# A graph layer and an LSTM on one core: one square root changes places with one copy in ScalarE's queue

## The chip, the cores and the metric

The kernel runs on one core of a Trainium2 chip. The core has five engines that each work through a queue of their own in order: TensorE (PE in the profile, its weight loads PEld), VectorE (DVE), ScalarE (ACT), GpSimd (POOL) and SyncE (SP). They wait for each other by semaphores. Transfers (DMA) are issued from the queues and run beside them. TensorE writes its results to PSUM, from where VectorE and ScalarE read them; all other tiles lie in SBUF.

The metric is the device time of one execution in microseconds (us), the median over the runs shown; less is better.

## The reference

`x` holds 1250 nodes with 512 features, `src` and `dst` 20000 edges, sorted by `dst`. A two-layer graph network on the normalised rows is added to `x`, then an LSTM that walks over the nodes in order:

```python
def _gcn2_layer(h, h0, src, dst, norm, w1, w2, b, layer):
    beta = float(np.log(LAMBDA / layer + 1.0))
    x = h * norm
    agg = jax.ops.segment_sum(x[src], dst, num_segments=h.shape[0])
    agg = agg * norm
    f = agg * (1.0 - ALPHA)
    f0 = h0 * ALPHA
    rst = (1.0 - beta) * f + beta * (f @ w1) + (1.0 - beta) * f0 + beta * (f0 @ w2) + b
    return jax.nn.relu(rst)
...
    h = feat @ fc_w.T + fc_b
    deg = jax.ops.segment_sum(jnp.ones_like(dst, dtype=h.dtype), dst, num_segments=n)
    norm = jnp.clip(deg, 1.0, None) ** (-0.5)
...
    x = x + _L0_gnn_ref(_layernorm(x, axis=-1), src, dst, ...)
    x = x + _L0_ffn_ref(_layernorm(x, axis=-1)[None], ...)[0]
```

`_layernorm` takes the mean off each row and divides by sqrt(var + 1e-5). What matters here is the beginning: the layer norm of `x`, the product `h` with `fc_w`, and the products of `h` with `w2` of both layers, which are the parts `f0 @ w2` and `(1 - beta) * f0 + b`.

## The kernel before

The 1250 rows are laid out as 10 tiles of 128 rows (T = 10, R = 128), each of 512 features.

The work has three stages. The *first stage* (L294 to L560, up to about 183 us in the profile) does two things side by side: it makes layer norm, `h` and the products with `w2` for each tile, and it counts the edges into an adjacency matrix. The *second stage* (`layers`, L797) is the aggregation with that matrix, twice. The *third* (`lstm`, L925) is the recurrence. The change touches the first stage alone.

In the first stage TensorE, VectorE and ScalarE carry out exactly the order in which the code is written (`tc.manual_schedule` at L341): on each engine an instruction starts only when all that were written before it for that engine have started, and when what it needs is there. The loop `for s in range(T + 3)` at L500 writes the stage in portions. One portion works on several tiles at different steps. Portion s = 4, the fifth, writes in this order (before the change):

- `transposed(...)` (L507): TensorE turns the normalised rows of tile 4 by four transposes into a PSUM tile (L169, `psT`), and ScalarE copies it to SBUF as `xT` (L174).
- `stats(5, 7)` and `scales(5, 7)` (L510, L511): VectorE takes mean and variance of tiles 5 and 6 (L157, L158) and adds eps (L162, `ln_v`); ScalarE takes the square root (L88, `ln_s`); VectorE refines its inverse in five small operations (L90 to L95) and makes `nmr`, minus the mean over the deviation (L354). `rsqrt` is at L84, its tiles are of their own for each call.
- `normed(5)` (L513): ScalarE writes the normalised rows of tile 5 (L362).
- `add_base(0)` (L517, L498): VectorE adds the biases to the two products of tile 0 with `w2`, from PSUM into `base1` and `x2`. The pool `psM` has two buffers, and both hold these products until then.
- `count(c0)` (L519): a batch of edges. For each group of 125 edges VectorE has made two one-hot tiles (L434, L436, eight buffers of each); TensorE multiplies them into a PSUM block (L450, with a first zero product L447 for a new block). VectorE makes the one-hots of a batch two batches on. A finished block is cast by ScalarE (L289).
- `product(..., fcT)` (L521, L180): TensorE multiplies `xT` of tile 3 with `fc_w` into the next buffer of `psM`, the one that held the first product of tile 0.
- further batches, the transposes and the copy of `h` of tile 2 (`hT`, L524), the bias of `h` (L526), and the two products of tile 1 with `w2` (L548, L554).

In portion s = 1 the same two calls stand at the same place for tiles 2 and 3. Portions 1 and 5 have further statistics behind their counts (L528). The sizes of the batches per portion are in `per_slot` (L486).

Of the kernel before, what the change touches and what calls it, by code (L numbers as in the profile page):

```python
# [38 lines left out]
def gnn_lstm_kernel(  # L39
# [115 lines left out]
    def layernorm_stats(pool, mv, t, rows):  # L155
        st = pool.tile([R, 6], F32, name="bnst")
        nc.vector.bn_stats(st, rows)  # L157
        nc.vector.bn_aggr(mv[:, t, :], st)  # L158

    def layernorm_scale(pool, mv, out, name, times=1.0):  # L160
        ve = pool.tile([R, mv.shape[1]], F32, name=name + "_v")
        nc.vector.tensor_scalar(ve, mv[:, :, 1], EPS, None, OP.add)  # L162
        rsqrt(pool, ve, out, name, times)
# [8 lines left out]
    def transposed(pool, ps, rows, name):  # L172
        o = pool.tile([128, KD, R], F32, name=name)
        nc.scalar.copy(o, transpose_in(ps, rows))  # L174
        return o

    def product(ps, lT, rhs, name="psM"):
        p = ps.tile([R, D], F32, name=name)
        for k in range(KD):
            nc.tensor.matmul(p, lT[:, k, :], rhs[:, k, :], start=(k == 0), stop=(k == KD - 1))  # L180
        return p
# [32 lines left out]
    with ExitStack() as gnn_stack:  # L214
# [20 lines left out]
        def most_edges():  # L235
            nc.vector.tensor_reduce(most, S.rearrange("b i r -> b (i r)"),
                                    mybir.AxisListType.X, OP.max)
            nc.vector.tensor_scalar(most, most, 256.0, None, OP.is_gt)

        def row_totals():  # L240
            nc.vector.tensor_reduce(row, deg, mybir.AxisListType.X, OP.add)
            nc.vector.tensor_sub(row, row, most)

        def total(pn):
            nc.tensor.matmul(pn, row, ones, start=True, stop=True)
            nc.vector.tensor_scalar(missing, pn, -1.0, float(E), OP.mult, OP.add)
# [38 lines left out]
        def close_block(p, i, dst):  # L285

            nc.scalar.copy(dst, p.rearrange("b (i q a) -> b a i q", i=T, a=T))  # L289
            nc.vector.tensor_reduce(S[:, :, 4 * i:4 * i + 4],  # L290
                                    dst.rearrange("b a i q -> b i q a"),
                                    mybir.AxisListType.X, OP.add)

        with tc.tile_pool(name="prep", bufs=1) as prep, \  # L294
# [46 lines left out]
            with tc.manual_schedule(engines={mybir.EngineType.PE, mybir.EngineType.DVE,  # L341
# [6 lines left out]
                def stats(t0, t1):  # L348
                    for t in range(t0, t1):
                        layernorm_stats(work, mv, t, xt[:, t, :])  # L350

                def scales(t0, t1):
                    layernorm_scale(prep, mv[:, t0:t1, :], rstd[:, t0:t1], f"ln{t0}")
                    nc.vector.scalar_tensor_tensor(nmr[:, t0:t1], mv[:, t0:t1, 0], -1.0,  # L354
                                                   rstd[:, t0:t1], op0=OP.mult, op1=OP.mult)
# [3 lines left out]
                def normed(t):  # L359
                    if t < T:  # L360
                        xns[t] = work.tile([R, D], F32, name="xn")
                        nc.scalar.activation(xns[t], xt[:, t, :], AF.Identity,  # L362
                                             bias=nmr[:, t:t + 1], scale=rstd[:, t:t + 1])
# [76 lines left out]
                def count_group(c):  # L440
                    lo, hi = spans[c]
                    ob, od = hot.pop(c)
                    done = []
                    for i in range(lo // BW, (hi - 1) // BW + 1):
                        if i not in blocks:
                            blocks[i] = acc.tile([R, D], F32, name="acc")[:, :BW * T]
                            nc.tensor.matmul(blocks[i], none[:, :R], none, start=True, stop=False)  # L447
                        d0, d1 = max(lo, i * BW), min(hi, (i + 1) * BW)
                        last = all((i + 1) * BW <= a for a, b in spans[c + 1:])
                        nc.tensor.matmul(blocks[i][:, (d0 - i * BW) * T:(d1 - i * BW) * T], ob,  # L450
                                         od[:, (d0 - lo) * T:(d1 - lo) * T],
                                         start=False, stop=last)
                        if last:
                            done.append((blocks.pop(i), i))
                    return done
# [5 lines left out]
                def onehots(n):  # L461
                    for c in range(n * BATCH, min((n + 1) * BATCH, EC)):
                        make_onehot(c)

                def count(batches):
                    nonlocal counted
                    for n in range(counted, counted + batches):
                        closed = []
                        for c in range(n * BATCH, (n + 1) * BATCH):
                            closed += count_group(c)  # L470
                        onehots(n + 2)
                        for p, i in closed:
                            close_block(p, i, adj[:, :, :, 4 * i:4 * i + 4])
                    counted += batches
# [15 lines left out]
                def scale_w2(l):  # L490
                    nc.scalar.activation(w2[l], w2[l], AF.Copy, scale=ALPHA * betas[l])

                def add_w2(l):
                    add_identity(w2[l], ALPHA * (1.0 - betas[l]))

                def add_base(t):
                    for l, p in enumerate(ps_b.pop(t)):
                        nc.vector.tensor_add(base[l][:, t, :], p, bl[l])  # L498

                for s in range(T + 3):  # L500
                    c0, c1, c2 = per_slot[s] if s < len(per_slot) else (0, 0, 0)
                    if 0 < s < 3:

                        ps_h[s - 1] = product(psM, xTs.pop(s - 1), fcT)
                        count(c0)
                    if 0 < s < T:
                        xTs[s] = transposed(work, psT, xns.pop(s), "xT")  # L507
                    if s in (1, 4):
                        t0 = 2 if s == 1 else 5
                        stats(t0, t0 + 2)  # L510
                        scales(t0, t0 + 2)  # L511
                    if s:
                        normed(s + 1)  # L513
                    if s == 2:
                        scale_w2(0)
                    if 0 <= s - 4 < T - 3:
                        add_base(s - 4)  # L517
                    if s >= 3:
                        count(c0)  # L519
                        if s - 1 < T:  # L520
                            ps_h[s - 1] = product(psM, xTs.pop(s - 1), fcT)  # L521
                    count(c1)
                    if 0 <= s - 2 < T:
                        hTs[s - 2] = transposed(prep2, psT, h[:, s - 2, :], "hT")  # L524
                    if 0 <= s - 1 < T:
                        nc.vector.tensor_add(h[:, s - 1, :], ps_h.pop(s - 1), fcb)  # L526
                    count(c2)
                    if s in (1, 5):  # L528

                        t0, t1 = (4, 5) if s == 1 else (7, T)  # L530
                        stats(t0, t1)
                        scales(t0, t1)
                    if s == 2:
                        scale_w2(1)
                        add_w2(0)
                        add_w2(1)
                    if 0 <= s - 3 < T:


                        hT = hTs.pop(s - 3)  # L540
                        ps, name = (psM, "psM") if s < T + 1 else (acc, "acc")
                        if s == T + 1:
                            total(psT.tile([128, KD, R], F32, name="psT")[:1, 0, :1])
                            split_first(prep2, order[3:7])
                        if s == T + 2:
                            add_base(T - 2)
                            split_first(prep2, order[7:9])
                        ps_b[s - 3] = [product(ps, hT, w2[0], name)]  # L548
                        if s == T:
                            most_edges()  # L550
                            count_edges(psT.tile([128, KD, R], F32, name="psT")[:, 0, :])
                            row_totals()
                            degree_norm(prep)
                        ps_b[s - 3].append(product(ps, hT, w2[1], name))  # L554
                        if s == T:
                            add_base(T - 3)
                            split_first(prep2, order[:3])
# [643 lines left out]
```

## Time and profile before

| | us |
|---|---|
| runs | 1070.84, 1070.83, 1069.89; median 1070.83 |
| profiled execution: its own time | 1068.22 |
| profiled execution: span from first to last instruction | 1066.3 |
| TensorE busy | 1002.9 |
| VectorE busy | 533.3 |
| ScalarE busy | 327.9 |
| mean granted TensorE clock | 0.992 |

A row of the timeline reads: start in us, duration in us, engine, line, operation, tile written <- tiles read, shape, number of instructions merged, and in brackets the idle time of the engine just before with the instruction that ended it. "The chain that ended last" is followed back from the end of the execution: at each step to what released an instruction, or to the instruction before it on its engine. Busy times of merged TensorE rows overlap by some tenths of a us with the next row, since matmuls are pipelined.

### The profile page before, as it was taken

The page shows a single profiled execution, that of the slowest core. Times are in us where ns is not written, and L with a number is a line of the kernel's source. Part 1 is how long each engine was busy: PE and PEld are TensorE (multiplying, and loading weights), DVE is VectorE, ACT ScalarE, POOL GpSimd, SP SyncE. Part 2 cuts the span into 40 slices and gives each one's busy share as a digit, 9 for nine tenths or more (in the row PEclk, how much of TensorE's full clock was granted, in tenths as well). Part 3 has the DMA queues.
Part 4 walks back from the last instruction along what each step waited for, and adds up shares of the span by engine and source line. Part 5 has one row for each costly group of instructions (what it writes and reads, how often), then busy time and mean ns, then how long its engine had stood idle before and what let it go on. Part 6 is the DMA issues. An engine that isn't in the chain of part 4 may idle for free.

```text
span 1066.3 us, 26042 instructions
## 1 busy us (share of the span) xinstructions
PE 1002.9 (94%) x10988; PEld 519.0 (49%) x10988; DVE 533.3 (50%) x1915; ACT 327.9 (31%) x1012; POOL 79.5 (7%) x119
## 2 busy tenths in 40 slices
PE   6899999999999999999999989999999999999996
PEld 4455554554455443344444444544544544454453
DVE  7888877003400665665555444444444444445444
ACT  3312224213410124443333333333333333333332
POOL 1100000520000001111010144000000000000000
PEclk9899999999999999999999999999999999999999
DMA  8200001600200045853333356333333333434441
GB/s 220 89 1 1 1 1 50 231 1 20 77 1 1 0 109 175 247 163 116 106 120 105 120 147 175 93 91 97 100 90 94 102 92 91 122 84 121 113 107 22
DMA packets 38223, 98.48 MB, mean 92 GB/s; under 512 B 5796, under 2 KB 11756, under 8 KB 38094
## 3 DMA queue, kind: packets, MB, share of 16 engines
q1 hardware_dynamic: 28208, 68.67, 23.9%
q0 software_dynamic: 7168, 23.60, 6.6%
q10 hardware_dynamic: 2718, 4.42, 1.6%
q8 instruction: 89, 1.46, 0.6%
q14 instruction: 40, 0.33, 0.1%
HBM read 74.29 MB, written 19.76 MB: 88 GB/s over the span
## 4 chain that ended last, share of the span: by engine, by line
PE 70%; DVE 14%; ACT 8%; issue 3%; DMA 3%; SPq 1%; POOL 0%; ACTq 0%; DVEq 0%; POOLq 0%
PE gates L654 30%; PE psM L180 15%; PE agg L816 12%; PE psM L1008 8%; ACT adj L661 3%; PE acc L450 3%; DVE adj L664 3%; ACT adj L672 3%; DVE hT L688 3%; DVE adj L667 2%; DVE adj L673 2%; DMA h<-xp_d 1%; PE gates L646 1%; DMA xp_d<-planes 1%; PE psT L169 1%
## 5 line engine op out<-in xcount | busy, mean ns | idle before, releaser
L654 PE MATMUL gates<-Wh,hT 128*32 128x256 f32 x7936 | 453.6, 380 | 38.4 <-DVE hT L688 38.4
L654 PEld LDWEIGHTS gates<-Wh,hT 128*32 128x32 f32 x7936 | 232.9, 109 | 230.8 <-DVE hT L688 78.6
L664 DVE SCALAR_TENSOR_TENSOR adj<-adj 128x128 f32<-128x128 f32 (+1 forms) x260 | 76.6, 295 | 215.0 <-ACT adj L661 215.0
L1008 PE MATMUL psM<-Wx,xT 128*128 128x512 f32 x320 | 147.7, 607 | 0.0
L661 ACT ACTIVATE adj<-gates 128x192 f32<-128x192 f32 x248 | 81.7, 329 | 207.6 <-PE gates L654 198.5
L816 PE MATMUL agg<-adj,planes 128*128 128x512 bf16 x720 | 130.1, 344 | 1.9 <-DVE x L498 1.9
L672 ACT ACTIVATE adj<-adj 128x64 f32<-128x64 f32 (+1 forms) x249 | 63.9, 257 | 126.0 <-DVE adj L667 126.0
L816 PEld LDWEIGHTS <-planes 128*128 128x128 bf16 x720 | 70.4, 98 | 62.4 <-DVE x L498 2.7
L673 DVE SCALAR_TENSOR_TENSOR adj<-adj 128x64 f32<-128x64 f32 (+1 forms) x249 | 56.3, 226 | 80.5 <-ACT adj L672 80.5
L1008 PEld LDWEIGHTS psM<-Wx,xT 128*128 128x128 f32 x320 | 58.6, 191 | 70.7 <-issue 70.0
L688 DVE STREAM_TRANSPOSE hT<-adj 128x64 f32<-128x64 f32 x248 | 60.9, 246 | 8.5
L667 DVE SCALAR_TENSOR_TENSOR adj<-adj 128x64 f32<-128x64 f32 (+1 forms) x260 | 59.4, 228 | 8.9
L180 PE MATMUL psM<-w,hT 128*128 128x512 f32 x128 | 58.6, 610 | 0.0
L1028 POOL DMA_DIRECT2D xp_d<-planes x40 | 29.2, 731 | 375.8 <-DVE planes L1027 232.8
L436 DVE TENSOR_SCALAR od<-ids,key 125x820 f16<-125x820 f16 (+42 forms) x160 | 56.9, 356 | 0.0
L663 ACT ACTIVATE adj<-gates 128x64 f32<-128x64 f32 x248 | 54.0, 218 | 0.0
L646 PE MATMUL gates<-h,sel 96*32 96x256 bf16 x992 | 49.9, 273 | 0.0
L450 PE MATMUL acc<-od,ob 125*128 125x400 f16 (+22 forms) x360 | 46.4, 260 | 3.0 <-DVE od L436 2.7
L434 DVE TENSOR_SCALAR ob<-ids,low 125x128 f16<-125x128 f16 x160 | 40.6, 254 | 10.3 <-PE acc L450 10.1
L646 PEld LDWEIGHTS <-sel 96*32 96x32 bf16 x992 | 26.5, 97 | 34.9 <-issue 15.9
L1020 ACT CAST planes<-adj 128x512 bf16<-128x512 f32 x40 | 24.7, 618 | 60.4 <-DVE adj L1018 60.4
L598 DVE SCALAR_TENSOR_TENSOR r<-psM,norm,base 128x512 f32<-128x512 f32 x10 | 7.5, 751 | 71.4 <-PE psM L180 71.4
(163 smaller groups left out, 720.4 us busy)
## 6 DMA issues: line engine op xcount, KB each, us to landing
h<-xp_d SPq DMA_DIRECT2D x136, 384.0 KB, 4.1
xp_d<-planes POOLq DMA_DIRECT2D x40, 384.0 KB, 3.5
base<-x POOLq DMA_DIRECT2D x40, 64.0 KB, 4.9
w<-in_L_gnn_w_dram SPq DMA_DIRECT2D x2, 1024.0 KB
w<-in_L_gnn_w_dram POOLq DMA_DIRECT2D x2, 1024.0 KB, 6.4
xp_d<-planes SPq DMA_DIRECT2D x10, 144.0 KB, 3.5
h<-in_x_dram SPq DMA_DIRECT2D x10, 128.0 KB, 2.7
h<-in_x_dram SPq DMA_DIRECT2D x10, 120.0 KB, 4.1
```

Of the source, the lines that this page charges most:

```text
L180: nc.tensor.matmul(p, lT[:, k, :], rhs[:, k, :], start=(k == 0), stop=(k == KD - 1))
L450: nc.tensor.matmul(blocks[i][:, (d0 - i * BW) * T:(d1 - i * BW) * T], ob, od[:, (d0 - lo) * T:(d1 - lo) * T], start=False, stop=last)
L646: nc.tensor.matmul(ps[s][32 * j:32 * (j + 1), :, :], lhs(j), rhs(j, s), start=True, stop=False)
L654: nc.tensor.matmul(ps[s][32 * j:32 * (j + 1), :, :], hT[b // 2][:, b % 2, :], Wh[:, b, :, 128 * j + 64 * s:128 * j + 64 * (s + 1)], start= ...
L661: nc.scalar.activation(cg[:, 1:4, :], p[:, 0:3, :], AF.Tanh, scale=0.25)
L664: nc.vector.scalar_tensor_tensor(pr, cg[:, 1:3, :], 1.0, cg[:, 0:4:3, :], op0=OP.add, op1=OP.mult)
L667: nc.vector.scalar_tensor_tensor(then[:, 0, :], pr[:, 0, :], 0.5, pr[:, 1, :], op0=OP.mult, op1=OP.add)
L672: nc.scalar.activation(th, cg[:, 0, :], AF.Tanh, scale=0.5)
L673: nc.vector.scalar_tensor_tensor(hh, so, 1.0, th, op0=OP.add, op1=OP.mult)
L688: nc.vector.transpose(hT.rearrange("p b c -> p (b c)"), hh[:, m])
L816: nc.tensor.matmul(p[:, :n * R], planes[:, k, pl, f * 128:(f + 1) * 128], adj[:, k, t0:t0 + n, :].rearrange("b i r -> b (i r)"), start=(k ...
L1008: nc.tensor.matmul(p, yT[n][:, k, :], quarter(Wx[:, k, :, :], j), start=(k == 0), stop=(k == KD - 1))
```

## The change

In portion s = 4 the calls `stats(5, 7)` and `scales(5, 7)` are written ahead of `transposed(...)` instead of behind it. In portion s = 1 nothing changes.

```diff
@@ -503,12 +503,15 @@
 
                         ps_h[s - 1] = product(psM, xTs.pop(s - 1), fcT)
                         count(c0)
+                    if s == 4:
+
+                        stats(5, 7)
+                        scales(5, 7)
                     if 0 < s < T:
                         xTs[s] = transposed(work, psT, xns.pop(s), "xT")
-                    if s in (1, 4):
-                        t0 = 2 if s == 1 else 5
-                        stats(t0, t0 + 2)
-                        scales(t0, t0 + 2)
+                    if s == 1:
+                        stats(2, 4)
+                        scales(2, 4)
                     if s:
                         normed(s + 1)
                     if s == 2:
```

The transposes are TensorE's, and the statistics VectorE's; ScalarE is the only engine that has work in both parts. So the two programs differ in one place of one queue, ScalarE's (besides line numbers):

```diff
 L174 TensorCopy hT<-psT 128x512
-L174 TensorCopy xT<-psT 128x512
 L88 Activation ln_s<-ln_v 128x2
+L174 TensorCopy xT<-psT 128x512
 L362 Activation xn<-base,nmr,rstd 128x512
```

Lines behind L516 have a number higher by 3 in the changed kernel.

## The prediction

> **What bounds the kernel now.** I read the page's busy times and slices first, then the shares of the chain that ended last.
>
> ```profile
> PE 1002.9 (94%) x10988; PEld 519.0 (49%) x10988; DVE 533.3 (50%) x1915; ACT 327.9 (31%) x1012; POOL 79.5 (7%) x119
> ...
> PE   6899999999999999999999989999999999999996
> ...
> PE 70%; DVE 14%; ACT 8%; issue 3%; DMA 3%; SPq 1%; POOL 0%; ACTq 0%; DVEq 0%; POOLq 0%
> ```
>
> TensorE is busy 94% of the span, so a step elsewhere counts only where TensorE stands still for it. The edit lies in the first stage, in the portion s = 4 of the loop at L500. Its place in time is where the fifth copy to xT (tile 4) and the square root of tiles 5 and 6 run, near 44 us. So the next view is the chain in order of time there (start, duration, what):
>
> ```profile
> 43.48 0.45 PE psT L169 x4
> ...
> 44.01 0.58 ACT xT L174
> 44.59 0.11 ACT ln_s L88
> ...
> 44.73 0.18 DVE ln_r L90
> ...
> 45.80 0.70 DVE base L498
> ...
> 46.54 3.70 PE psM L180 x8
> ```
>
> This is the whole case: for 2.6 us the chain leaves TensorE. It goes from the transposes through ScalarE's copy and the square root, through VectorE's six small operations (L90 to L354), then the sum of `base`, and only then back to a product. The timeline of all engines shows who stood idle, in brackets:
>
> ```profile
> 42.19 0.17 DVE L162 TENSOR_SCALAR ln_v<-mv 128x2 f32<-128x2 f32 x1
> ...
> 44.01 0.58 ACT L174 COPY xT<-psT 128x512 f32<-128x512 f32 x1 [7.42 <-PE psT L169]
> 44.13 0.42 PE L450 MATMUL acc<-od,ob 125*128 125x20 f16 x5
> 44.49 0.21 ACT L88 ACTIVATE ln_s<-ln_v 128x2 f32<-128x2 f32 x1
> 44.73 0.17 DVE L90 RECIPROCAL ln_r<-ln_s 128x2 f32<-128x2 f32 x1 [2.37 <-ACT ln_s L88]
> ...
> 46.54 3.70 PE L180 MATMUL psM<-fcT,xT 128*128 128x512 f32 x8 [1.99 <-DVE base L498]
> ```
>
> The input of the square root (ln_v, L162) is ready at 42.36. ScalarE is idle then, but the head of its queue is the copy, which waits for transposes that TensorE begins only at 43.31. VectorE waits 2.37 us for a square root that could have run, and TensorE 1.99 us for VectorE: the product of tile 3 writes the PSUM buffer that the sum into `base` (add_base(0), L498) still has to read, since psM has two.
>
> **The change part by part.** Nothing is added or removed. On TensorE, VectorE, GpSimd and SyncE every instruction keeps its place. On ScalarE alone the square root of tiles 5 and 6 (L88) goes from behind the copy to xT to in front of it. The moved lines issue no DMA and pass no queue but ScalarE's.
>
> *The square root earlier.* Where nothing stands before it, it follows ln_v at once, as tiles 7 to 9 show:
>
> ```profile
> 74.34 0.17 DVE L162 TENSOR_SCALAR ln_v<-mv 128x3 f32<-128x3 f32 x1
> ...
> 74.78 0.17 DVE L90 RECIPROCAL ln_r<-ln_s 128x3 f32<-128x3 f32 x1 [0.27 <-ACT ln_s L88]
> ```
>
> From the start of ln_v to the reciprocal that is 0.44 us. So the reciprocal moves from 44.73 to 42.19 + 0.44 = 42.63, by 2.10 us. From there to the product VectorE's work is unchanged (44.73 to 46.54, 1.81 us), so the buffer is free at 44.44 instead of 46.54. The sum into `base` would start at 43.70; the matmuls it reads are the first half of the sixteen that ran from 36.60 to 43.48, done near 40.0. The second sum, into x2, would start at 44.31, after 43.48 as it must.
>
> *TensorE.* It has work of its own (the counts of L450) to 44.13 + 0.42 = 44.55. So the product starts when both are done. By the gate alone the gain is 2.10. By the recorded idle time it is 1.99. By the chain without a stop (the next tile's product, 60.81 to 64.30, takes 3.49 from the end of the counts) the product would end at 48.04 instead of 50.25 (46.54 + 3.70 in the chain): 2.21. Ends 1.99 and 2.21; I take 2.10, which lies between and is set by the gate.
>
> *The copy behind the square root.* This is the added wait: queued behind the square root on ScalarE are the copy to xT, the scaled rows of tile 5 (L362), the cast at 50.70 and the copy to hT at 52.08. The square root would run from 42.40 to 42.61, in idle time of ScalarE, 1.3 us before the transposes are done, so the copy still starts at 44.01 and the price is nothing. If that cover went (statistics late by more than 1.4 us), the copy's reader is the product at 60.64, sixteen us later, so it would still cost nothing. The rows of tile 5 move from 45.98 to about 44.5; they are transposed at 59.3.
>
> *New neighbours.* The sum into `base` now runs beside the copy to xT, both reading PSUM. No row has just this pair. The sum took 0.69 beside the scaled rows at 45.80 and 0.68 alone at 56.54. I bound it at -0.01 and +0.1 us (a hundredth between those rows, times ten for the untried pair) and take 0.
>
> *What is late next.* From 46.54 to 167 TensorE has no wait worth a line; VectorE waits for it instead (1.81 us at 50.41, 2.32 at 59.54, 1.88 at 64.53), so it can follow 2.10 us earlier. DMA share is 0.00 to 0.01 between 36 and 160 us, so no transfer with a time of its own can hold the shift. The weights of later stages are requested when the last planes are written (GpSimd waited 145.8 us for those), so they shift too.
>
> *The clock.* TensorE's granted clock in stretches (columns: stretch, its length, busy times by engine, clock, DMA share, GB/s):
>
> ```profile
> 25.00:30.00 5.00, 2.41 (x13) 1.81 (x14) 4.56 (x24) 4.71 (x6) 1.59 (x4) 0.54 1.05 390
> 30.00:32.00 2.00, 2.00 (x4) 0.97 (x4) 2.00 (x9) 2.00 (x3) 1.63 (x5) 0.50 1.03 370
> ...
> 44.00:48.00 4.00, 2.01 (x12) 1.03 (x10) 3.10 (x14) 1.50 (x3) 0.00 (x0) 1.00 0.00 2
> 48.00:52.00 4.00, 4.00 (x28) 2.46 (x27) 2.19 (x13) 0.49 (x1) 0.00 (x0) 1.00 0.00 0
> ```
>
> A stop of 2.18 us before 26.82 was followed by half clock to 32; the stop of 1.99 us in our portion was not followed by any. At half clock a product of eight takes 5.25 (at 161.77) instead of 3.49: 1.76 more. So in this execution the clock adds 0 to the gain. The Trainium skill, "TensorE: Matmul & The Clock Gate" (What's actually happening), states that the clock is halved after an idle window of about 3.4 us, that the window runs freely, and that where the work falls in it varies from run to run. The trace agrees in that half clock and full clock both follow stops of about 2 us; by that rule the stop would cost the clock in some executions and not in others.
>
> *Sum.* 2.10 + 0 + 0 + 0 = 2.10 us. The profiled execution took 1068.22 us (span 1066.3 and 1.92 around it) and would take 1066.1, its span 1064.2. The median of the runs, 1070.83, is 2.61 above it; I take the same difference off the median: 1070.83 - 2.10 = 1068.7.
>
> **The rivals.**
>
> 1. *The stop costs the clock too.* If in the usual execution half clock follows the stop at 44.55, it goes with the stop: 1070.83 - 2.10 - 1.76 = 1067.0. For: the same length of stop did it at 26.8, and the runs are 2.6 us above the execution whose clock held. Against: the clock row at 44 to 52 is 1.00.
> 2. *Given back later, or never had.* One more half-clock product behind the change (there is one at 161.77, where 20 matmuls of one column ran before it) costs 1.76 of the 2.10: 1070.5. Or the square root does not start earlier: 1070.8. Against the latter: it writes a tile of its own and reads only ln_v.
> 3. *Slower: the aggregation stage entered cold.* TensorE stops 1.90 us before 183.40, and the change shifts this stop by 2.1 us against whatever sets the clock. Half clock there costs half its length. A stretch as long as that from 25.7 to 32.1 costs 3.2, time 1071.9; it decides from 4.2 us on (slower than before), and slower by 0.2% needs 8.5 us. For: stops of this length have been followed by half clock. Against: the longest stretch in the trace is 6.4 us, and full clock holds from 183 to 376.
> 4. *Slower by ScalarE's queue*: the square root holds the copy to xT. It starts to cost when the statistics end later than about 58 us (the product at 60.64, less 2.1 and the copy's 0.58). Every us behind that costs one, and 1073.0 would need them near 62, twenty us late, while VectorE works without a break from 34.79 to 42.36. Hardly possible.
>
> **How the numbers follow.** What a measurement of this kernel tells from no change is about 0.2%, 2.14 us: just what I forecast, so the first two classes split the main case. Main case (gap closes, 1068.7, own range 1068.0 to 1069.4 from the ends 1.99 and 2.21 and half a us of scatter between runs, which lie 0.9 apart): 0.70. Rival 1: 0.14; 2: 0.11; 3: 0.04; 4: 0.01. Faster by over 0.2%: 0.40 of the main case, as its bound of 2.21 lies beyond the line, and rival 1, together 0.54. Within 0.2%: the other 0.30 and rival 2, 0.41. Slower: 0.05. The range takes in rival 1 and the weaker part of rival 2, 1066.8 to 1070.2, and leaves out the full giving back, the slower cases and the tails.
>
> **What would show it.** Right: the square root of tiles 5 and 6 starts 0.2 us after ln_v and 1.3 us before the copy; the reciprocal's wait of 2.37 falls to about 0.3; TensorE's wait of 1.99 for `base` falls under 0.15; the product ends 2.1 us earlier relative to the transposes of tile 4; and the aggregation's first matmul comes as much earlier. Wrong: the wait for `base` stays, or a new one of about 2 us appears between 46 and 183 us, or the aggregation starts earlier and the end does not.

## The result, and the profile after

The changed kernel took 1066.96 us (median of 20 runs, 1063.32 to 1070.56), the kernel before 1070.03 us (20 runs, 1067.34 to 1074.06). The ratio is 0.9976 with a 95% interval of 0.9965 to 0.9987, so 2.6 us faster, between 1.4 and 3.7. The prediction was 1068.7 within 1066.8 to 1070.2, faster by 2.10 us.

The profiled execution of the changed kernel took 1065.37 us, its span is 1063.3 us. Busy times, slices and chain shares of its page:

```profile
PE 1001.9 (94%) x10988; PEld 519.2 (49%) x10988; DVE 532.9 (50%) x1915; ACT 327.6 (31%) x1012; POOL 79.5 (7%) x119
...
PE   7999999999999998999999989999999999999996
...
PE 71%; DVE 14%; ACT 7%; DMA 3%; issue 3%; SPq 1%; POOL 0%; ACTq 0%; DVEq 0%; POOLq 0%
```

No engine has less work; one wait is gone. The chain in order of time at the place of the change (start, duration, what) no longer leaves TensorE:

```profile
43.50 0.44 PE psT L169 x4
43.94 0.21 PE acc L450 x2
44.15 0.17 PE acc L447
44.32 0.26 PE acc L450 x5
44.58 3.59 PE psM L180 x8
48.16 0.94 PE acc L450 x11
```

The timeline of the changed kernel shows why:

```profile
42.21 0.17 DVE L162 TENSOR_SCALAR ln_v<-mv 128x2 f32<-128x2 f32 x1
42.41 0.20 ACT L88 ACTIVATE ln_s<-ln_v 128x2 f32<-128x2 f32 x1 [5.80 <-DVE ln_v L162]
...
42.65 0.17 DVE L90 RECIPROCAL ln_r<-ln_s 128x2 f32<-128x2 f32 x1 [0.27 <-ACT ln_s L88]
...
43.72 0.69 DVE L498 TENSOR_TENSOR base<-psM,b 128x512 f32<-128x512 f32 x1
...
44.03 0.58 ACT L174 COPY xT<-psT 128x512 f32<-128x512 f32 x1 [1.41 <-PE psT L169]
44.15 0.42 PE L450 MATMUL acc<-od,ob 125*128 125x20 f16 x5
44.33 0.68 DVE L498 TENSOR_TENSOR x<-psM,b 128x512 f32<-128x512 f32 x1
...
44.46 3.70 PE L180 MATMUL psM<-fcT,xT 128*128 128x512 f32 x8
```

The square root starts 0.20 us after ln_v and 1.6 us before the copy, VectorE's wait for it falls from 2.37 to 0.27 us, and the product of tile 3 has no wait in brackets at all. From the first transpose of tile 4 to the end of the product of tile 3 it is 4.66 us (43.50 to 48.16); before it was 6.77 (43.48 to 50.25). That is 2.11 us.

The aggregation starts at 179.60 us instead of 183.40, by 3.80 us. 2.09 of these are the change; most of the rest is a product behind it: the eight passes that took 5.25 us at 161.77 before take 3.56 at 159.69. The clock in stretches tells (columns: stretch, its length, busy times by engine, granted clock, DMA share, GB/s). Before:

```profile
156.00:160.00 4.00, 4.00 (x15) 1.89 (x14) 3.97 (x6) 1.07 (x3) 0.00 (x0) 1.00 0.00 0
160.00:164.00 4.00, 4.00 (x19) 2.58 (x20) 2.67 (x13) 0.41 (x2) 0.00 (x0) 0.74 0.02 4
164.00:168.00 4.00, 4.00 (x13) 1.93 (x12) 1.52 (x3) 1.14 (x2) 0.00 (x0) 0.84 0.00 0
```

After:

```profile
156.00:160.00 4.00, 4.00 (x25) 2.91 (x24) 3.12 (x6) 0.00 (x0) 0.00 (x0) 1.00 0.01 4
160.00:164.00 4.00, 4.00 (x15) 2.01 (x14) 2.73 (x12) 1.55 (x3) 0.00 (x0) 1.00 0.00 0
```

So one pair of executions mixes the change with the clock. From the aggregation to the end the two are alike: 882.9 us before, 883.7 after. Two questions are left for the experiments: is it really the held PSUM buffer, and does the stop cost the clock as well (the first rival)?

### The profile page after: what moved, and what is told of

Its sections match the earlier page's. It is cut to its first block, busy times and chain, and to the rows that moved or that the text cites. A ratio compares the mean times of both kernels' runs of the same rounds, so it can differ in the third digit from the quotient of the medians.

```text
span 1063.3 us, 26042 instructions
## 1 busy us (share of the span) xinstructions
PE 1001.9 (94%) x10988; PEld 519.2 (49%) x10988; DVE 532.9 (50%) x1915; ACT 327.6 (31%) x1012; POOL 79.5 (7%) x119
## 4 chain that ended last, share of the span: by engine, by line
PE 71%; DVE 14%; ACT 7%; DMA 3%; issue 3%; SPq 1%; POOL 0%; ACTq 0%; DVEq 0%; POOLq 0%
PE gates L657 30%; PE psM L180 14%; PE agg L819 12%; PE psM L1011 8%; ACT adj L664 3%; PE acc L450 3%; DVE adj L667 3%; ACT adj L675 3%; DVE hT L691 3%; DVE adj L670 2%; DVE adj L676 2%; DMA h<-xp_d 1%; DMA xp_d<-planes 1%; PE gates L649 1%; DMA base<-in_x_dram 1%
```

## The experiments

The runs used several chips, so each ratio is against runs of the kernel before on the same chip. Four experiments (sums first, square root held back, stop filled, portion 1 too) share one chip and its runs of the kernel before; the changed kernel itself was not run on that chip, so a comparison with it is one of ratios from two chips. "Section" is the time from the first transpose of tile 4 to the end of the product of tile 3, by the chain or the timeline of the run's profile.

**The sums first, the square root left where it was.**

```diff
                         stats(t0, t0 + 2)
+                        if s == 4:
+                            add_base(0)
                         scales(t0, t0 + 2)
...
-                    if 0 <= s - 4 < T - 3:
+                    if 0 < s - 4 < T - 3:
                         add_base(s - 4)
```

> The kernel before, with the square root left behind the copy to xT; instead the two sums of tile 0 (add_base(0)) are written between the statistics and the scales of portion 4, so VectorE does them before it waits for the square root. Theory (the price of the old order is the PSUM buffer that the sum into base holds): the sum runs near 42.2 us, the product of tile 3 follows the counts without a stop, TensorE's idle 1.99 us goes, the product ends 2.1 us earlier against the transposes of tile 4, and the time falls as with the change, by 2.1 us (0.2%). The square root still starts about 44.5 and the rows of tile 5 about 46. Rival (the gain came from the rows of tile 5 or from ScalarE's order): no gain, 1070.

Measured: ratio 0.9959 (0.9941 to 0.9977), 4.4 us faster (2.5 to 6.3), so more than the 2.1 us expected. Its timeline:

```profile
42.51 0.67 DVE L498 TENSOR_TENSOR base<-psM,b 128x512 f32<-128x512 f32 x1
...
44.44 0.59 ACT L174 COPY xT<-psT 128x512 f32<-128x512 f32 x1 [7.42 <-PE psT L169]
...
44.57 0.43 PE L450 MATMUL acc<-od,ob 125*128 125x20 f16 x5
...
44.83 3.66 PE L180 MATMUL psM<-fcT,xT 128*128 128x512 f32 x8
44.92 0.21 ACT L88 ACTIVATE ln_s<-ln_v 128x2 f32<-128x2 f32 x1
```

The square root still runs behind the copy, the rows of tile 5 start at 46.41 as late as ever, and yet TensorE's stop is gone; the section is 4.58 us. So TensorE's stop in the old order came from the buffer that the sum into `base` holds, and from nothing else that hangs on the square root. Why the whole time fell by more than the stop is not shown by this run.

**The square root held back in the new order.** Three passes of ScalarE stand between ln_v and the square root.

```diff
-                        scales(5, 7)
+                        scales(5, 7, [xt[:, 5, :]] * 3)
...
+        for n, r in enumerate(rows):
+            nc.scalar.activation(h[:, 7 + n, :], r, AF.Identity, bias=v[:, 0:1])
         nc.scalar.activation(s, v, AF.Sqrt)
```

> The changed kernel with three extra passes of ScalarE over a tile between ln_v and the square root (each 0.8 us, 0.71 from start to start; they write rows of h that are overwritten later). Theory (each us of the square root is a us of TensorE): the square root starts 2.13 us later, near 44.55, the product of tile 3 starts near 46.6, TensorE's stop is back at 2.0 us, and the time is that of the kernel before (within 0.2%), although the order is that of the changed kernel. Rival (the order matters by itself, or the gain was luck of the clock): the time stays that of the changed kernel, 2 to 2.6 us under before.

```profile
43.18 0.17 DVE L164 TENSOR_SCALAR ln_v<-mv 128x2 f32<-128x2 f32 x1
43.39 1.95 ACT L88 ACTIVATE h<-base,ln_v 128x512 f32<-128x512 f32 x3 [5.80 <-DVE ln_v L164]
...
45.24 0.19 ACT L90 ACTIVATE ln_s<-ln_v 128x2 f32<-128x2 f32 x1
...
47.27 1.98 PE L182 MATMUL psM<-fcT,xT 128*128 128x512 f32 x4 [1.72 <-DVE base L500]
```

The three passes took 1.85 us instead of 2.13, and the product starts 4.09 us after ln_v instead of 2.25 in the changed kernel: 1.84 later. So at this place each us of the square root is a us of TensorE, and the order by itself does not close the stop. The whole time was a miss: expected like before, measured 0.9973 (0.9957 to 0.9989), 2.9 us faster (1.2 to 4.6), with a stop of 1.72 us where before has 1.99. That is the time that the rival named. The profile speaks against the order as its cause, since the stop is back; a stop that is 0.27 us shorter and that no half clock follows would give about 1 us by the estimate below, near the lower end of the interval. The rest stays open.

**The stop filled in the old order.** TensorE multiplies the identity while it waits.

```diff
                         count(c0)
+                        if s == 4:
+                            p = psT.tile([128, KD, R], F32, name="psT")
+                            for n in range(8):
+                                nc.tensor.matmul(p[:, 0, :], ident, ident, start=True, stop=True)
```

> The kernel before, with eight products of the identity with itself written behind the counts of portion 4, into a free PSUM buffer: TensorE works through its stop of 1.99 us, and nothing else moves. Theory (the wait itself is the price): the product of tile 3 still starts near 46.5, the time is that of before within 0.1%. Rival (the stop costs the clock): the mean granted clock rises and the time falls by up to 1.8 us, without the product of tile 3 starting earlier.

Measured, by the chain (first and third row) and the timeline:

```profile
44.62 0.45 PE psT L169 x4
45.53 2.01 PE L523 MATMUL psT<-ident 128*128 128x128 f32 x16
47.68 3.70 PE psM L180 x8
```

The product starts no earlier (section 6.76 us, as before; a product of the identity is two rows of the profile, so eight are x16), but the ratio is 0.9974 (0.9959 to 0.999), 2.8 us faster (1.1 to 4.4), and the mean granted clock of the runs is 0.9925 against 0.9906 of before on that chip. This is the rival's sign, though more than its 1.8 us, which the interval holds. The theory that the time stays within 0.1% falls.

**The kernel before, profiled three more times.**

> The kernel before once more, for its profile: does half clock follow the stop of portion 4 in some executions? So far filling the stop raised the mean granted clock from 0.9906 to 0.9925, about 4 us less at half clock, although the product of tile 3 started no earlier. The clock record shows stretches of 3.41 us on a grid that lies anew in each execution. Theory A (the stop costs the clock where one stretch of the grid holds most of it): in about half of the executions a stretch at half clock begins between 46.5 and 50 us and costs up to 1.7 us. Theory B (the stop never costs the clock, the means differ by scatter): full clock from 36 to 60 in all.

> As for the run ahead of it: theory A expects a stretch at half clock between 46.5 and 53 us in about half of these executions, theory B in none. The place of the grid in this execution is read from its other stretches.

> As for the two runs ahead of it: theory A expects a stretch at half clock behind the stop in about half of these executions, theory B in none.

All three had half clock behind the stop. The stretches of the first of them (columns as above), and its product of tile 3:

```profile
44.00:47.00 3.00, 1.08 (x13) 0.80 (x10) 1.57 (x8) 1.19 (x3) 0.00 (x0) 1.00 0.00 0
47.00:50.00 3.00, 2.93 (x4) 1.38 (x5) 2.13 (x10) 0.31 (x1) 0.00 (x0) 0.51 0.01 3
50.00:53.00 3.00, 3.00 (x15) 1.43 (x15) 0.38 (x2) 0.09 (x1) 0.00 (x0) 0.92 0.00 0
```

```profile
44.66 0.42 PE L450 MATMUL acc<-od,ob 125*128 125x20 f16 x5
47.07 5.38 PE L180 MATMUL psM<-fcT,xT 128*128 128x512 f32 x8 [1.99 <-DVE base L498]
```

5.38 us instead of 3.70: 1.68 us more, and the section is 8.45, 8.47 and 8.47 us in the three. The record of the clock in each trace consists of stretches of 3.41 us on a grid that lies anew in each execution. With the grid and TensorE's busy time, the profiles of kernels with a stop in portion 4 sort themselves:

| profile | stop, us | stretch of the grid with most of it | idle in that stretch | clock in the next stretch | product of tile 3 |
|---|---|---|---|---|---|
| before | 44.55 to 46.54 | 42.4 to 45.8 | 1.29 | 1.0 | 3.70 |
| before, again (1) | 45.08 to 47.07 | 43.7 to 47.1 | 1.99 | 0.5 | 5.38 |
| before, again (2) | 46.0 to 48.0 | 45.6 to 49.0 | 1.99 | 0.5 | 5.40 |
| before, again (3) | 45.9 to 47.9 | 45.3 to 48.7 | 1.99 | 0.5 | 5.40 |
| old order with early fill (below) | 43.7 to 45.7 | 43.1 to 46.5 | 1.99 | 0.5 | 5.40 |
| square root held back | 45.55 to 47.27 | 44.6 to 48.0 | 1.72 | 1.0 | 3.70 |

In these rows the stop costs the clock when one stretch holds all of its 1.99 us, and not when it is divided. For this stop the bound lies between 1.72 and 1.99 us idle of 3.41. The same count over all fourteen profiles of this case, from 7 us on, says how far that reaches. Of the stretches at full clock in which TensorE was idle for 1.94 us or more, 28 of 28 were followed by half clock; of those with 1.58 to 1.91 us, 4 of 19; of those with less, 4 of 4230. So between 1.58 and 1.91 us the idle time alone does not decide. Two cases (the first two rows are of the kernel before, the others of the kernel with the sums first):

```profile
21.95:25.36 3.41, 1.82 (x17) 1.21 (x15) 3.00 (x14) 1.10 (x3) 0.00 (x0) 1.00 1.04 344
25.36:28.78 3.42, 1.72 (x9) 1.29 (x10) 3.25 (x20) 3.37 (x4) 0.37 (x1) 0.50 1.06 390
...
176.61:180.03 3.42, 1.52 (x5) 0.46 (x4) 3.40 (x7) 1.86 (x3) 0.00 (x0) 1.00 0.88 295
180.03:183.44 3.41, 3.36 (x19) 1.81 (x21) 1.21 (x2) 0.62 (x1) 1.63 (x3) 1.00 0.39 54
```

A stretch idle for 1.59 us between transposes and counts was followed by half clock, and one idle for 1.90 us beside a product of 512 columns was not. If the grid lies evenly against the stop of portion 4, which no run shows, one stretch holds enough of it in (3.41 - 1.99) / 3.41 = 42% of the executions at least, and in (3.41 + 1.99 - 2 x 1.72) / 3.41 = 57% at most. This is an estimate. The profile that the prediction was made from is one with the stop divided. The Trainium skill, "TensorE: Matmul & The Clock Gate" (What's actually happening), gives the window as 3413 ns, free-running, and the half clock after an idle window; length and grid agree with the traces, but no window had to be idle throughout: 1.99 us of it sufficed. An idle window of 3.4 us does not fit into a stop of 2 us, so the prediction's step from that rule to a cost in some executions did not follow from the rule; that the cost came is shown by these traces.

**The same exchange in portion 1 as well.**

```diff
-                    if s == 4:
-
-                        stats(5, 7)
-                        scales(5, 7)
+                    if s in (1, 4):
+                        t0 = 2 if s == 1 else 5
+                        stats(t0, t0 + 2)
+                        scales(t0, t0 + 2)
...
-                    if s == 1:
-                        stats(2, 4)
-                        scales(2, 4)
```

> The changed kernel with the same exchange in portion 1 as well (statistics and square root of tiles 2 and 3 ahead of the copy of tile 1 to xT). There the statistics end later than the transposes: the square root ran at 20.63, the copy at 17.92. Theory (what counts is which input is late and who waits behind): the copy moves to about 20.8, the product of tile 1 from 18.55 to about 21.4, a new stop of 2.9 us for TensorE; its later stop of 2.18 us at 24.6 to 26.8, which waits for VectorE, swallows most of it, so 0 to +2.4 us against the changed kernel, most likely +0.5. Rival (a square root earlier is always good): faster than the changed kernel.

TensorE in this kernel, from its timeline:

```profile
21.35 5.21 PE L180 MATMUL psM<-fcT,xT 128*128 128x512 f32 x8 [3.39 <-ACT xT L174]
26.40 0.27 PE L450 MATMUL acc<-od,ob 125*128 125x40 f16 x4
...
27.57 0.69 PE L450 MATMUL acc<-od,ob 125*128 125x90 f16 x4
...
29.42 3.64 PE L180 MATMUL psM<-fcT,xT 128*128 128x512 f32 x8
```

The new stop came as expected (3.39 us, the product of tile 1 at 21.35), and the later stop swallowed it. But the sign was missed: 0.9951 (0.9934 to 0.9968) against before, no slower than the changed kernel by its ratio of 0.9976. Half clock came behind the new stop instead (21.0 to 24.4 us, the product of tile 1 took 5.21 us). TensorE, late by then, works through the time of its later stop, no half clock follows there, and the product of tile 2 takes 3.64 us instead of the 5.01 in the profile of the changed kernel. In this kernel half of the chain between 13 and 36 us (51%) runs over VectorE's one-hot tiles, in the changed kernel 20%. This suggests that a stop of TensorE there costs through the clock rather than through its length; the run does not part the two.

**An early stop filled.** This follows from it: in portion 2 of the changed kernel TensorE stops before the counts of the next batch. `keep_awake(n)` multiplies the identity with itself n times into a spare PSUM tile; the kernel before calls it already, at its start.

```diff
                         hTs[s - 2] = transposed(prep2, psT, h[:, s - 2, :], "hT")
+                    if s == 2:
+                        keep_awake(8)
```

> The changed kernel with eight products of the identity with itself written in portion 2 behind the transposes of h of tile 0, where TensorE stops for about 2.2 us (24.6 to 26.8) and half clock follows for 3.4 to 6.8 us. If half clock is set by how idle a stretch was, the stretches at half clock between 25 and 36 us become fewer, the product of tile 2 near 29.9 takes 3.6 instead of 4.8 to 5.9 us, and the time falls by 1 to 2 us against the changed kernel. If VectorE sets the pace there (the counts wait for its one-hot tiles until 29.6), less than 0.5 us.

Measured: 1063.2 us against 1068.16 of before on that chip, 0.9946 (0.9932 to 0.9961). TensorE's timeline and the clock:

```profile
24.48 1.95 PE L377 MATMUL acc<-ident 128*128 128x128 f32 x16
26.65 1.16 PE L450 MATMUL acc<-od,ob 125*128 125x90 f16 x4 [0.22 <-DVE od L436]
...
29.71 3.64 PE L180 MATMUL psM<-fcT,xT 128*128 128x512 f32 x8
```

```profile
20.00:25.00 5.00, 4.13 (x27) 2.62 (x26) 4.30 (x21) 1.10 (x3) 0.00 (x0) 1.00 1.03 351
25.00:30.00 5.00, 3.48 (x26) 2.69 (x26) 4.68 (x23) 5.00 (x6) 1.70 (x4) 1.00 1.06 387
30.00:36.00 6.00, 5.81 (x33) 3.16 (x32) 6.00 (x30) 2.65 (x5) 2.31 (x5) 1.00 0.22 70
```

With two us of useless work the clock stays at 1.00, and the section begins at 42.46 instead of 43.50 us. The grid of that execution alone doesn't explain it: in all four profiles with this fill the section begins between 42.46 and 42.65 us, in the nine without it that have portion 1 as before between 43.48 and 44.94. By the median this is the fastest kernel of the study; its interval overlaps that of the exchange in both portions.

**The change on top of the early fill.** With the early fill in place, the old order was measured with the early fill alone, with both stops filled, and the new order beside them.

```diff
                         hTs[s - 2] = transposed(prep2, psT, h[:, s - 2, :], "hT")
+                    if s == 2:
+                        keep_awake(8)
```

> The early fill of portion 2 (eight products of the identity) on the kernel before, so with the old order and its stop in portion 4. Theory (the old order costs 2.10 us of stop, and 1.69 us more in the executions where half clock follows the stop): the time lies 2.1 us above the changed kernel with the same fill when the clock holds and 3.8 when not; with half clock in about three of four executions, 3.4 us, about 1066.5. Rival (the fill takes over what the change gained, since TensorE is no longer late): within 1 us of the changed kernel with the fill.

> The kernel before with both fills: portion 2, and the stop of portion 4. The old order's stop is kept in length but can't cost the clock any more. Theory: 2.10 us above the changed kernel with the early fill, and 1.3 us under the old order with the early fill alone; in the profile the product of tile 3 still ends 6.8 us after the transposes of tile 4 begin. Rival (the whole gain was the clock): no slower than the changed kernel with the early fill.

> The changed kernel with the early fill, again beside the two others on one chip, as their measure: about 1063.2 if the chip is as fast as the last one, and no half clock between 20 and 60 us.

> The changed kernel itself beside the others on one chip: 2.1 us plus 1.69 us times the share of executions with half clock behind the stop under the kernel before, so 3.0 to 3.8 us (0.28 to 0.36%), and in its profile full clock from 36 to 60 us.

| on one chip | median us | ratio to before (1069.26) | section in the profile |
|---|---|---|---|
| old order, early fill | 1066.93 | 0.9974 (0.9958 to 0.999) | 8.46 |
| old order, both stops filled | 1066.09 | 0.9978 (0.9963 to 0.9992) | 6.76 |
| new order, early fill | 1063.8 | 0.995 (0.9936 to 0.9964) | 4.67 |
| new order, no fill | 1068.11 | 0.9988 (0.9971 to 1.0006) | 4.67 |

The sections are as expected to 0.1 us: 2.09 us for the stop and 1.70 for the clock. In the whole time, with the early fill, the new order is 2.6 and 3.0 us better than the two old ones by the ratios (3.1 and 2.3 by the medians). So with both stops filled the wait alone still costs, near the 2.10 us expected, and the rival that the whole gain was the clock falls. The difference between the two old ones, 1.3 us expected, is lost in the scatter: the ratio of the filled one is no better (0.9978 against 0.9974), its median is 0.8 us lower. The changed kernel alone was 1.3 us faster than before, with an interval from 3.1 faster to 0.6 slower; 3.0 to 3.8 was expected. That range lets half clock follow the stop in half to all of the executions, which is more than the estimate above. The early fill gained more than the 1 to 2 us expected, 1063.8 against 1068.11 us; the profiled execution without it took 1064.1, so the profiles don't show where the others lost their time.

## Why the prediction was right, and the term that was too small

*The square root earlier: right.* The forecast was 42.63 for the reciprocal and 44.44 for the free buffer; the profile has 42.65 and a product that starts at 44.46. The section is 4.66 to 4.68 us in five profiles of kernels with the new order and no delay, against 6.76 to 6.77 in three of the old order at full clock: 2.10 us, the value taken between 1.99 and 2.21.

*TensorE's own work, the copy behind the square root, the new neighbours: right.* The copy started at 44.03 instead of 44.01; the sum into `base` took 0.69 beside it, as alone within 0.01. The copy to `xT` was not held behind the square root, so the fourth rival did not appear.

*What is late next: right.* The first matmul behind the product came 2.09 us earlier (48.16 against 50.25), VectorE still waits 1.81 us for TensorE there (at 48.33), and no new wait stands between 46 and 183 us. The third rival did not appear either: the aggregation's stop of 1.89 us before 179.60 was not followed by half clock, and neither was it in any of the other thirteen profiles, even where one stretch held 1.90 us of it.

*The clock: the term that was mis-sized.* "So in this execution the clock adds 0 to the gain" was true at this stop, and the step from it to the median was the mistake: 0 was carried over to executions that the profile did not show. One reading beside it was off as well: the half clock that the prediction puts behind the stop before 26.82 began at 25.36, within that stop, behind the stretch idle for 1.59 us shown above, and it lasted 6.83 us, not 6.4. Four of five profiles with the full stop lost 1.68 to 1.70 us more. With the estimate of 42 to 57% of executions the term is 0.7 to 1.0 us, and the forecast would have been 2.8 to 3.1 us. The first rival had the mechanism right and its price of 1.76 nearly so; its chance of 0.14 treated as a property of the kernel what is drawn anew in each execution.

*The whole time.* 2.6 us (1.4 to 3.7) holds both 2.1 and 3.1, and the second measurement, 1.3 us, pulls towards 2.1. So the clock's share is shown in the section, in four profiles. In the whole time it is not settled: the filled stop gained 2.8 us with nothing earlier, more than the 1.7 us that one stretch at half clock costs, and filling it on top of the early fill gained nothing that the scatter lets through. Executions of one kernel lie up to 8.7 us apart. Most of that scatter goes with the clock: in the 20 runs of the changed kernel time falls by 0.94 us for each 0.001 of mean granted clock, with a correlation of -0.87. Which stretches those runs lost that have a clock of 0.989 stays open, as they have no profile.

*The range.* 1066.96 lies in it by 0.16 us, at its lower end, on the side of the first rival. That is in part luck: the forecast of 1068.7 started from the median of three runs, 1070.83, where twenty have 1070.03, and the range was widened for the first rival. The forecast's 2.10 us fits the section to 0.01 us; the whole time can't confirm it that closely.

## What to carry to other kernels

Where an engine's queue holds an instruction whose input is ready behind one whose input is late, look for who waits for the first; here one exchange closed a stop of 2 us on the bounding engine, and moving VectorE's sums did the same, because the thing awaited was a PSUM buffer. Before calling a reorder good, compare when the two inputs come in that place and what bounds there: in portion 1 the same exchange made a stop of 3.4 us, and it cost nothing in the end because a later stop went with it. Take the price of a TensorE stop from more than one profile: its length is the same in each, the half clock behind it is not, and where the stop can't be closed, useless products in it are worth a try.

## What the runs showed that was not expected

Useless work made the kernel faster: eight products in portion 2 together with the change gave 0.9946 and 0.995, where the change alone had 0.9976 and 0.9988, and eight in the stop of the old order gave 0.9974 with nothing earlier, though not measurably so on top of the early fill. The granted clock is a record of 3.41 us stretches, and in this case 1.94 us idle or more in one of them brought half clock in the next every time, less than 1.58 us almost never. The four exceptions show that a busy TensorE is not enough: each of these stretches held, to within 0.05 us, all of a run of 20 matmuls of one column each, which count as 2.4 us of busy time in the profile. In the ten other profiles the run reached over the end of a stretch, by 0.23 us or more, and no half clock followed.
